# A hand-written step order, chosen anew: each batch's scores placed next to a context product on TensorE

## The chip, the cores and the metric

The kernel runs on one core of one Trainium2 chip. The metric is the device time of one launch in microseconds (us). Three runs of the kernel before took 2436.83, 2435.96 and 2436.95 us; the median is 2436.83. The profile comes from one more execution, which took 2435.67 us as a whole and 2433.9 us from its first to its last instruction (the span).

## What is computed

The input is x, 128 batches of 128 rows and 512 columns, and one 128x128 matrix adj for each batch, all in 32-bit floats. Two layers follow each other:

```
h = relu(layernorm(x))
q, k, v = h Wq + bq, h Wk + bk, h Wv + bv          # 8 heads of 64
attn = softmax((q k^T) / 8 * (2 adj))              # 8 matrices of 128x128 a batch
x = x + (attn v) Wo + bo

h = relu(layernorm(x))
e[i, j] = leaky_relu(h W a_left [i] + h W a_right [j])
att = softmax over i of (e where adj > 0.5, else -9e15)
x = x + elu(att (h W))
```

## The kernel before

**Pairs, groups and units.** The work is cut into 64 pairs of two batches, a and b. Two pairs make a group of four batches; q, k and v are made for a whole group at once. A product with a 512x512 matrix is done in quarters by a scheme with seven block products in the place of eight, with sums and differences of blocks made ahead on VectorE (DVE). For a group this gives 21 *units* (seven each for v, q and k; function `product`, matmuls on line 261), which are spread over two rounds: U1 to U10 of an even pair are v0 v1 v2 v3 v4 q0 v5 q1 v6 q2, U1 to U11 of an odd pair are q3 q4 k0 q5 k1 q6 k2 k3 k4 k5 k6. Some units are read out at once: by a copy or bias step on ScalarE (ACT), called F with the unit's number (lines 273 and 278), or by an add on the DVE, called A (line 282). All units of v (or q, or k) that use bank "a" write the same accumulator one after another, so the next one must wait until the F step has read it. The products of a pair's rows with Wo (steps o0 to o6) and with W (w0 to w6) go the same way on line 302; they are read out by the steps od (DVE, line 400), zc (ACT, line 478) and wd (DVE, line 482).

**The attention of a batch** (letter a or b at the end of the name): `sc` makes the scores on TensorE: 8 products with a contraction of 64, on one half of the array's rows each (line 323; tile 64x128). `at` multiplies them with adj (DVE, line 329), `mx` takes the maxima (line 336), `ex0` to `ex3` are the exponentials of two heads each (ACT, line 341), `rc` the reciprocals (DVE, line 345), `nm0` to `nm3` the normalisation (ACT, line 350). `fl` transposes 32x32 blocks (DVE, line 357), `bl` and `pl` send the blocks out and bring them back in their places by DMA (SyncE's queue, lines 361 and 367), so that `pc` can make the context on TensorE: 8 products with an output of 64 partitions, on one half of the array's columns each (line 386; tile 128x64). `pe` copies the context to SBUF (ACT, line 393), and `cs0` to `cs3` make its block sums (DVE).

**The second layer of a pair:** statistics `st0`, `st1` (DVE), the power `pw` on GpSimd, `nm` (DVE, line 410), the normalised rows `h20`, `h21` (ACT, line 416), four dot products `d00` to `d11` (DVE, line 423), their spread by a transpose `pb` on TensorE (line 432), the mask `wm` (DVE, line 438), `pr`, `m1`, `e1`, `sw` for the softmax, the gather products `g0`, `g1` on TensorE (line 464), their copies `ge0`, `ge1` (ACT, line 470), block sums `gs0` to `gs3` (DVE), then w0 to w6, and at the end `ez`, `fa`, `fb` and the store `so`. The hidden rows of later pairs are made on the DVE by `hd0`, `hd1` and, for a group, the four block sums `hs0` to `hs3` (function `hidden_sum`). `t0`, `t1` and `s0` are the statistics of a later pair's x; `la`, `lt`, `lx`, `l0`, `lT` and `f0` are loads.

**Buffers that matter here.** Six PSUM buffers (pool `ps1`) are shared by the accumulators of the units, the row products, pc, pg and pb; the scores have two banks of their own in one buffer (`ps2`). There is one buffer each for `at`, `tr` and `aT`. A new tile in a buffer waits until the old tile there has been read.

**What sets the order.** Nothing is scheduled by the machine: the list `ORDER` (line 536) is written out, 138 of its steps exist, and each carries a lag. Round p goes through the list from left to right and runs each step for pair p minus its lag, if that step exists for that pair (entries with strange lags, such as A7:-37, are steps that exist for no pair). Each engine works through its own instructions in just this order, and waits where an input isn't ready. So the list sets the order on all engines, and a software pipeline over some five rounds:

```python
for p in range(early, N + late):
    for step, lag in ORDER:
        pair = p - lag
        for do in tables.get(pair, {}).get(step), first_use.get((pair, step)):
```

Of the kernel before, what the change touches and what calls it, by code (L numbers as in the profile page):

```python
# [24 lines left out]
def kernel(  # L25
# [35 lines left out]
    xs, x0s, adjs, adjTs, hAs, hSs = {}, {}, {}, {}, {}, {}  # L61
# [93 lines left out]
    def token_sum(h, s, k):  # L155

        if k == 0:
            nc.vector.tensor_tensor(s[:, 0], h[:, 2], h[:, 3], OP.add)
        elif k == 1:
            nc.vector.tensor_tensor(s[:, 1], s[:, 0], h[:, 0], OP.subtract)  # L160
        elif k == 2:
            nc.vector.tensor_tensor(s[:, 2], h[:, 0], h[:, 2], OP.subtract)
        else:
            nc.vector.tensor_tensor(h[:, 2], h[:, 1], s[:, 1], OP.subtract)
# [16 lines left out]
    st0, rows0, qks, vs, scs, ats, trs, blocks, aTs, pcs = ({} for _ in range(10))  # L181
# [45 lines left out]
            nc.vector.scalar_tensor_tensor(h, h, 0.0, row, op0=OP.max, op1=OP.mult)  # L227

    def hidden_sum(g, k):
        if k == 0:  # L230
            hSs[g] = grp.tile([P, 3, 2, 2 * S], F32, name="hS")
        token_sum(hAs[g], hSs[g], k)

# [288 lines left out]
    def spread_u():  # L522
# [13 lines left out]
    ORDER = [  # L536
        (step.split(":")[0], int(step.split(":")[1]))
        for step in """
        w5:4 o4:2 ata:0 U2:0 w6:4 mxa:0 sw:3 pca:1 od4:2 plb:1 g0:3 zc5:4 o5:2 od4c:2 wd6:4 o6:2 fa:4 exa2:0 hs1:1
        g1:3 exa0:0 ez:4 F2:0 U1:0 ge0:3 U8:1 fb:4 exa1:0 ge1:3 od5:2 od6:2 rca0:0 exa3:0 st0:2 st1:2 gs0:3 t0:0  # L540
        rca1:0 w0:3 nma1:0 U4:0 w1:3 gs2:3 scb:0 pw:2 pcb:1 so:4 A3:20 nm:2 pea:1 t1:0 nma0:0 gs1:3 nma2:0 nma3:0
        gs3:3 zc0:3 h21:2 A8:1 A9:1 fla:0 U11:1 atb:0 h20:2 hs3:1 F4:0 mxb:0 peb:1 F1:0 U3:0 d10:2 o0:1 A11:1 F3:0
        d11:2 A7:-37 A2:0 U5:0 cs0:1 exb0:0 A10:28 f0:0 cs1:1 lT:0 lt:2 exb1:0 F5:0 exb2:0 A4:21 exb3:0 U6:0 rcb0:0
        nmb0:0 F6:0 wd1:3 U7:0 A5:0 F8:-10 F7:0 o1:1 F11:10 cs2:1 l0:-1 d00:2 hd0:0 rcb1:0 s0:0 A1:19 nmb1:0 w2:3
        hd1:0 nmb3:0 zc2:3 pb:2 U9:0 F9:0 hs0:0 lx:1 o3:1 A6:0 d01:2 w4:3 nmb2:0 wm:2 sh:1 bla:0 od0:1 la:-1 pr:2
        U10:0 w3:3 od1:1 o2:1 F10:0 hs2:0 pla:0 flb:0 m1:2 zc4:3 od2:1 sca:-1 blb:0 cs3:1 e1:2 wd4c:3
        """.split()
    ]

    def steps(p):  # L550
# [60 lines left out]
        if odd and (g + 2) * 2 < N:  # L611
            for k in range(4):
                table[f"hs{k}"] = lambda k=k: hidden_sum(g + 2, k)
# [11 lines left out]
    with tc.manual_schedule():  # L625
# [10 lines left out]
        for k in range(4):  # L636
            hidden_sum(0, k)
        for n, u in enumerate(SEQ):
            firsts, adds = product(0, u[0], int(u[1]))
            if n == 2:  # L640
                weight_sums(wq_sb)
            if n == 4:
                first_stats(2)
            if n == 6:
                hidden_T(2, rows[2], "h2")
            if n == 8:
                weight_sums(wk_sb)
            if n == 10:
                first_stats(3)
            if n == 12:  # L650
                hidden_T(3, rows[3], "z")
                load_x0(4)
            if n == 14:
                for k in range(4):
                    hidden_sum(1, k)
            firsts()
            adds()
# [59 lines left out]
```

## Time and profile before

| engine | busy us | share of the 2433.9 us | instructions |
|---|---|---|---|
| TensorE, matmuls (PE) | 2395.6 | 98% | 14264 |
| TensorE, weight loads (PEld) | 2055.1 | 84% | 14264 |
| VectorE (DVE) | 1993.2 | 82% | 3909 |
| ScalarE (ACT) | 1449.3 | 60% | 4811 |
| GpSimd (POOL) | 180.3 | 7% | 323 |

In the profile, PE is TensorE's matmul stream and PEld its weight loads, which run beside it. Each 32-bit matmul shows as two instructions, so a unit of four matmuls is counted x8 and a row product of two x4. The DMA engines are busy 42.7% of the time with the kernel's transfers. The granted TensorE clock is 0.996 of full speed on the mean.

The run has three parts: the head up to some 80 us, in which the first group's products are made and the first pair is worked on alone; rounds of 37.1 us each on the mean; and a tail from about 2326 us, in which no units are left. The first scores of the last pair start at 2350.71 us.

### The profile page before, as it was taken

The numbers are of one execution on the slowest core, as the hardware profiler recorded it, in microseconds if no ns is written. First come the engines' busy times: TensorE is split into PE (matmuls) and PEld (weight loads), VectorE is DVE, ScalarE is ACT, GpSimd is POOL, SyncE is SP. The second block draws the span as 40 slices with busy tenths as digits, with TensorE's granted clock in tenths as the row PEclk, the third lists the DMA queues.
The fourth block names the chain that finished last, engine by engine and source line by source line (L and its number), as shares of the span: only waits on it lengthen the run. The fifth ranks groups of instructions, "written<-read, shape, count | busy, mean of one in ns | idle before, by whom it ended". The sixth has DMA issues, their size and how long they took to land.

```text
span 2433.9 us, 40532 instructions
## 1 busy us (share of the span) xinstructions
PE 2395.6 (98%) x14264; PEld 2055.1 (84%) x14264; DVE 1993.2 (82%) x3909; ACT 1449.3 (60%) x4811; POOL 180.3 (7%) x323
## 2 busy tenths in 40 slices
PE   8999999999999999999999999999999999999987
PEld 7788888888888888888888888888888888888876
DVE  5788888888888888888888888888888888887786
ACT  2566556656565665565665656655656655666573
POOL 1000000000000000000000000000000000000000
PEclk9999999999999999999999999999999999999998
DMA  4435434445343454344453434453444544443331
GB/s 156 122 110 147 129 115 119 137 135 139 113 132 109 142 140 143 101 135 121 135 148 111 133 109 138 135 145 99 139 118 135 148 118 125 116 140 116 104 112 65
DMA packets 255275, 306.09 MB, mean 126 GB/s; under 512 B 21856, under 2 KB 181600, under 8 KB 254432
## 3 DMA queue, kind: packets, MB, share of 16 engines
q1 hardware_dynamic: 251568, 303.37, 42.7%
q8 instruction: 112, 1.84, 0.3%
q14 instruction: 91, 0.75, 0.1%
q0 software_dynamic: 1920, 0.13, 0.1%
q10 hardware_dynamic: 1584, 0.01, 0.0%
HBM read 202.64 MB, written 100.79 MB: 125 GB/s over the span
## 4 chain that ended last, share of the span: by engine, by line
PE 96%; DVE 2%; ACT 1%; issue 0%; DMA 0%; POOL 0%; SPq 0%; POOLq 0%; DVEq 0%; ACTq 0%
PE acc_a L261 27%; PE row_a L302 23%; PE acc_c L261 14%; PE row_c L302 9%; PE acc_b L261 7%; PE sc L323 6%; PE pc L386 5%; PE pg L464 5%; PE pb L432 1%; DVE junk L423 0%; DVE nmx L336 0%; PE pt L202 0%; ACT at L341 0%; DVE st L172 0%; DMA x<-in_x 0%
## 5 line engine op out<-in xcount | busy, mean ns | idle before, releaser
L341 ACT ACTIVATE at<-at,nmx 128x128 f32<-128x128 f32 x1024 | 398.6, 394 | 90.7 <-DVE nmx L336 90.6
L302 PE MATMUL row_a<-w,gT 128*128 128x256 f32 x1280 | 338.5, 388 | 15.1 <-DVE z L482 14.2
L350 ACT ACTIVATE at<-at,rs 128x128 f32<-128x128 f32 x1024 | 331.8, 394 | 0.0
L302 PE MATMUL row_a<-wo,cxT 128*128 128x256 f32 x1280 | 328.8, 380 | 0.1
L302 PEld LDWEIGHTS row_a<-w,gT 128*128 128x128 f32 x1280 | 239.3, 191 | 55.6 <-issue 9.2
L478 ACT COPY z<-row_a 128x256 f32<-128x256 f32 x256 | 94.9, 371 | 301.0 <-PE row_a L302 298.6
L302 PEld LDWEIGHTS row_a<-wo,cxT 128*128 128x128 f32 x1280 | 237.8, 190 | 30.8 <-DVE x L400 0.7
L400 DVE TENSOR_TENSOR x<-row_a,x 128x256 f32<-128x256 f32 x320 | 134.9, 422 | 144.5 <-PE row_a L302 139.8
L329 DVE SCALAR_TENSOR_TENSOR at<-sc,adj 128x1024 f32<-128x1024 f32 x128 | 156.8, 1225 | 98.5 <-PE sc L323 97.3
L278 ACT ACTIVATE kT<-acc_a,bk 128x256 f32<-128x256 f32 x256 | 107.5, 471 | 178.4 <-PE acc_a L261 178.4
L176 POOL TENSOR_SCALAR mv<-mv 128x2 f32<-128x2 f32 x128 | 32.8, 256 | 2196.3 <-ACT at L341 1858.8
L341 ACT ACTIVATION_READ_ACCUMULATOR at<-at,nmx 128x1 f32 x1024 | 195.3, 191 | 0.0
L278 ACT ACTIVATE qT<-acc_a,bq 128x256 f32<-128x256 f32 x256 | 105.7, 463 | 123.6 <-PE acc_a L261 123.6
L172 DVE BATCH_NORM_STATS2 st<-x 128x6 f32<-128x512 f32 x256 | 172.6, 674 | 4.7 <-DMA x<-in_x 4.6
L357 DVE STREAM_TRANSPOSE tr<-at 128x1024 f32<-128x1024 f32 x128 | 158.1, 1235 | 8.4 <-ACT at L350 8.3
L323 PEld LDWEIGHTS sc<-kT,qT 64*128 64x128 f32 x2048 | 124.2, 187 | 42.5 <-issue 42.1
L336 DVE TENSOR_REDUCE nmx<-at 128x8 f32<-128x1024 f32 x128 | 155.9, 1218 | 3.3
L323 PE MATMUL sc<-kT,qT 64*128 64x128 f32 x2048 | 148.7, 285 | 0.0
L464 PE MATMUL pg<-w,h 128*128 128x128 f32 x1024 | 141.2, 281 | 0.0
L464 PEld LDWEIGHTS pg<-w,h 128*128 128x128 f32 x1024 | 129.2, 191 | 14.0 <-issue 10.6
L386 PE MATMUL pc<-aT,v 128*64 128x128 f32 x2048 | 140.1, 279 | 0.0
L273 ACT COPY v<-acc_a 128x512 f32<-128x512 f32 x128 | 75.2, 587 | 104.2 <-PE acc_a L261 103.6
(126 smaller groups left out, 4925.4 us busy)
## 6 DMA issues: line engine op xcount, KB each, us to landing
blocks<-tr SPq DMA_DIRECT2D x128, 512.0 KB, 3.6
aT<-blocks SPq DMA_DIRECT2D x512, 128.0 KB, 2.9
x<-in_x SPq DMA_DIRECT2D x123, 512.0 KB, 6.6
out<-x SPq DMA_DIRECT2D x64, 512.0 KB, 3.8
hA<-in_xT SPq DMA_DIRECT2D x120, 256.0 KB, 4.6
mr<-rows SPq DMA_DIRECT2D x60, 256.0 KB, 4.7
adj<-in_adj SPq DMA_DIRECT2D x64, 128.0 KB, 5.2
adjT<-in_adjT SPq DMA_DIRECT2D x64, 128.0 KB, 4.3
```

The lines of the kernel that those rows point to most:

```text
L172: nc.vector.bn_stats(st, src[:, i, :])
L261: nc.tensor.matmul(acc[:, m, :], lhsT, rhs, start=fresh and m == 0 and c == 0, stop=c == 1, skip_group_check=True)
L278: nc.scalar.activation(dst(t, f)[:, m, :], a[:, m, :], AF.Identity, bias=bias[:, j : j + 1])
L302: nc.tensor.matmul(acc, left[:, la, c, :], w[:, wb, c, :], start=n in (0, 3) and c == 0, stop=c == 1, skip_group_check=True)
L323: nc.tensor.matmul(sc[:, s * C + j, :], qT[r, j, cols], kT[r, j, cols], start=True, stop=True)
L329: nc.vector.scalar_tensor_tensor(at, scs.pop(b), QSCALE, adjs[p][:, i : i + 1, :].to_broadcast([P, H, S]), op0=OP.mult, op1=OP.mult)
L336: nc.vector.tensor_reduce(nmx, at, AX.X, OP.max, negate=True)
L341: nc.scalar.activation(at[:, j, :], at[:, j, :], AF.Exp, bias=nmx[:, j : j + 1], accum_out=sums[:, j : j + 1])
L350: nc.scalar.activation(at[:, j, :], at[:, j, :], AF.Copy, scale=rs[:, j : j + 1])
L357: nc.vector.transpose(trs[b], at.rearrange("p h (j k) -> p j h k", k=Q))
L386: nc.tensor.matmul(pc[s * D : (s + 1) * D, j, :], vs[b // G][:, b % G, head * D : (head + 1) * D], aT[:, :, s * C + j, :], start=True, sto ...
L464: nc.tensor.matmul(pg[:, c, :], h1s[p][0][:, i, c * P : (c + 1) * P], wts[p][:, i, :], start=True, stop=True)
```

## The change

Two things change in the file. `hidden_sum` now makes its tile when the group has none, and no longer at k = 0, so that the four block sums may begin in any order that the list has. And the whole list is another one:

```diff
     def hidden_sum(g, k):
-        if k == 0:
+        if g not in hSs:
             hSs[g] = grp.tile([P, 3, 2, 2 * S], F32, name="hS")
@@
-        w5:4 o4:2 ata:0 U2:0 w6:4 mxa:0 sw:3 pca:1 od4:2 plb:1 g0:3 zc5:4 o5:2 od4c:2 wd6:4 o6:2 fa:4 exa2:0 hs1:1
-        g1:3 exa0:0 ez:4 F2:0 U1:0 ge0:3 U8:1 fb:4 exa1:0 ge1:3 od5:2 od6:2 rca0:0 exa3:0 st0:2 st1:2 gs0:3 t0:0
-        rca1:0 w0:3 nma1:0 U4:0 w1:3 gs2:3 scb:0 pw:2 pcb:1 so:4 A3:20 nm:2 pea:1 t1:0 nma0:0 gs1:3 nma2:0 nma3:0
-        gs3:3 zc0:3 h21:2 A8:1 A9:1 fla:0 U11:1 atb:0 h20:2 hs3:1 F4:0 mxb:0 peb:1 F1:0 U3:0 d10:2 o0:1 A11:1 F3:0
-        d11:2 A7:-37 A2:0 U5:0 cs0:1 exb0:0 A10:28 f0:0 cs1:1 lT:0 lt:2 exb1:0 F5:0 exb2:0 A4:21 exb3:0 U6:0 rcb0:0
-        nmb0:0 F6:0 wd1:3 U7:0 A5:0 F8:-10 F7:0 o1:1 F11:10 cs2:1 l0:-1 d00:2 hd0:0 rcb1:0 s0:0 A1:19 nmb1:0 w2:3
-        hd1:0 nmb3:0 zc2:3 pb:2 U9:0 F9:0 hs0:0 lx:1 o3:1 A6:0 d01:2 w4:3 nmb2:0 wm:2 sh:1 bla:0 od0:1 la:-1 pr:2
-        U10:0 w3:3 od1:1 o2:1 F10:0 hs2:0 pla:0 flb:0 m1:2 zc4:3 od2:1 sca:-1 blb:0 cs3:1 e1:2 wd4c:3
+        atb:1 mxb:1 A1:74 f0:1 gs2:4 A2:1 lT:1 U3:1 h20:3 bla:1 A3:55 gs3:4 A11:2 o0:2 h21:3 d01:3 peb:2 lx:2 F3:1
+        d10:3 exb1:1 w2:4 exb0:1 lt:2 U5:1 F5:1 rcb0:1 U6:1 U7:1 cs2:2 d00:3 cs0:2 exb2:1 zc2:4 exb3:1 pb:3 A5:1
+        rcb1:1 d11:3 wm:3 hd0:1 cs1:2 nmb1:1 w4:4 hd1:1 U8:1 nmb3:1 sh:2 nmb2:1 F7:1 nmb0:1 hs0:1 U9:1 F4:1 A6:1 w3:4
+        o1:2 F6:1 od0:2 zc4:4 pr:3 F9:1 s0:1 pla:1 A7:-33 l0:0 U10:1 w5:4 od1:2 F8:11 m1:3 wd4c:4 F10:1 flb:1 blb:1
+        o2:2 w6:4 e1:3 sca:0 od2:2 cs3:2 pca:1 o4:2 sw:3 wd6:4 F11:3 o3:2 A9:1 pea:1 zc5:4 ata:0 mxa:0 g0:3 od4:2 U2:0
+        ez:4 o5:2 exa3:0 la:0 exa0:0 plb:1 exa2:0 fa:4 ge0:3 hs1:1 od4c:2 g1:3 fb:4 rca1:0 F2:0 od5:2 hs2:1 st0:2
+        exa1:0 nma3:0 A8:1 ge1:3 o6:2 A4:26 rca0:0 w0:3 od6:2 t1:0 w1:3 U1:0 hs3:1 nma0:0 zc0:3 t0:0 A10:84 st1:2
+        nma2:0 nma1:0 gs0:3 so:4 U11:1 scb:0 gs1:3 pw:2 pcb:1 wd1:3 U4:0 fla:0 nm:2 F1:0
```

The two lists begin at different places of a round, so they are easier to compare when each is turned to begin at sca, with lags counted from there. TensorE's steps are then:

```
before: sca w5:4 o4:2 U2 w6:4 pca:1 g0:3 o5:2 o6:2 g1:3 U1 U8:1 w0:3 U4 w1:3 scb pcb:1 U11:1 U3 o0:1 U5 U6 U7 o1:1
        w2:3 pb:2 U9 o3:1 w4:3 U10 w3:3 o2:1
after:  sca pca:1 o4:2 o3:2 g0:3 U2 o5:2 g1:3 o6:2 w0:3 w1:3 U1 U11:1 scb pcb:1 U4 U3 o0:1 w2:3 U5 U6 U7 pb:2 w4:3
        U8 U9 w3:3 o1:1 U10 w5:3 o2:1 w6:3
```

Before, pcb stood behind scb while sca and pca had other products between them; after, both contexts stand right behind scores. U8 runs in its pair's own round and no longer one round later, and w5 and w6 stand at the end of a round where they stood at the start of the next. On the other engines the steps change places as well. The DVE's steps from one sca to the next, after the change, are: od2 cs3 sw wd6 A9 ata mxa od4 fa hs1 od4c fb rca1 od5 hs2 st0 A8 rca0 od6 t1 hs3 t0 st1 gs0 gs1 wd1 fla nm atb mxb gs2 A2 gs3 A11 d01 d10 rcb0 cs2 d00 cs0 A5 rcb1 d11 wm hd0 cs1 hd1 sh hs0 A6 od0 od1 m1 wd4c flb; before, wd1 stood behind d10, d11 and rcb0, and nm ahead of fla. Those of ACT are: pea zc5 ez exa3 exa0 exa2 ge0 F2 exa1 nma3 ge1 nma0 zc0 nma2 nma1 F1 h20 h21 peb F3 exb1 exb0 F5 exb2 zc2 exb3 nmb1 nmb3 nmb2 F7 nmb0 F4 F6 zc4 pr F9 F10 e1; before, too, peb stood behind h20 and h21. What each step computes stays the same.

## The prediction

> **What bounds the kernel now.** I read the page first: TensorE's busy share, then the chain that ended last.
>
> ```profile
> PE 2395.6 (98%) x14264; PEld 2055.1 (84%) x14264; DVE 1993.2 (82%) x3909; ACT 1449.3 (60%) x4811; POOL 180.3 (7%) x323
> ...
> PE 96%; DVE 2%; ACT 1%; issue 0%; DMA 0%; POOL 0%; SPq 0%; POOLq 0%; DVEq 0%; ACTq 0%
> ```
>
> The chain is TensorE for 96% of the span, so only TensorE's own time counts, unless another engine makes it wait. Next, TensorE's waits over the whole run:
>
> ```profile
> PE row_a L302 <- DVE z L482: 14.2, 5, 5.0
> PE pt L202 <- DVE hn L196: 9.1, 2, 8.8
> PE acc_a L261 <- ACT v L273: 5.4, 2, 4.7
> ```
>
> Asked by window, the first of these falls after 2340 us and the others before 130 us. The stretch between is free of waits: the stretches table shows TensorE busy for 74.00 us of every 74, and the timeline repeats every 74.18 us for two rounds (37.09 a round). So there are three parts: a head to about 80 us, 61 rounds bound by TensorE, and a tail from 2326 us.
>
> What a step costs in the middle is read from the difference of two starts, since ends are modelled. Here are TensorE's pieces in one round (start, length, engine, line, operation, count):
>
> ```profile
> 1175.80 1.03 PE L302 MATMUL row_a<-wo,cxT 128*128 128x256 f32 x4
> 1176.76 1.16 PE L323 MATMUL sc<-kT,qT 64*128 64x128 f32 x16
> 1177.85 1.13 PE L302 MATMUL row_a<-w,gT 128*128 128x256 f32 x4
> 1178.82 1.03 PE L302 MATMUL row_a<-wo,cxT 128*128 128x256 f32 x4
> 1179.68 1.89 PE L261 MATMUL acc_a<-hS,wq 128*128 128x256 f32 x8
> 1181.41 1.03 PE L302 MATMUL row_c<-w,gT 128*128 128x256 f32 x4
> 1182.36 1.09 PE L386 MATMUL pc<-aT,v 128*64 128x128 f32 x16
> 1183.39 1.16 PE L464 MATMUL pg<-w,h 128*128 128x128 f32 x8
> 1184.38 1.03 PE L302 MATMUL row_a<-wo,cxT 128*128 128x256 f32 x4
> ...
> 1193.05 1.03 PE L302 MATMUL row_a<-w,gT 128*128 128x256 f32 x4
> 1194.01 1.16 PE L323 MATMUL sc<-kT,qT 64*128 64x128 f32 x16
> 1195.10 1.09 PE L386 MATMUL pc<-aT,v 128*64 128x128 f32 x16
> 1196.12 1.99 PE L261 MATMUL acc_a<-hA,wk 128*128 128x256 f32 x8
> 1197.95 1.03 PE L302 MATMUL row_a<-wo,cxT 128*128 128x256 f32 x4
> ```
>
> The reader is to see: a row product normally takes 0.86 us (1178.82 to 1179.68) and a unit of line 261 takes 1.73. A row product ahead of scores takes 0.96 (1175.80), one behind scores 0.97 (1177.85), one ahead of a context 0.95 (1181.41), and the gather behind a context 0.99 where the other gather of the round takes 0.89. So each border between a full-array product and sc or pc costs 0.10. The second half of the round, where pcb already follows scb, has 0.10 at each outer border and none between: sc 1.09, pc 1.02.
>
> **What the Trainium skill says.** "TensorEngine Tiling (Array Packing)", Key Properties, says that "Changing tiling mode (not just tile) drains the TensorE". The trace agrees that a change costs: 64x128 (sc) and 128x64 (pc) beside 128x128 show the 0.10 above. It doesn't show that all changes cost alike: from sc to pc is a change of mode too, yet pc behind sc starts as late after sc (1.09) as a row product does, and itself loses nothing more. "TensorE: Matmul & The Clock Gate", Step-by-step, says that the next weights are loaded while the present matmul runs. The trace agrees: a row product's weights start 0.2 us ahead of its matmuls, but those of sc, pc and the product behind them start together with theirs.
>
> **The change part by part.** No instruction is added or removed; the new condition in hidden_sum only lets the sums stand in another order. Everything else is place in the queues.
>
> (1) sca and pca meet. Before, apart: 0.10+1.09+0.10 and 0.10+1.03+0.10, 2.52 us. After, like scb and pcb: 0.10+1.09+1.02+0.10, 2.31. That is 0.20 us a round; 61 TensorE-bound rounds give **-12.2**. In the two rounds after, TensorE isn't the bound, so nothing is counted.
>
> (2) The wait of U5 on F3. In even rounds the copy F3 (line 273) ends as U5, v's next unit into the same accumulator, wants to write. Before, one row product stood between U3 and U5, and U5 took 1.81 (1162.55 to 1164.36; two rounds on 1.80) instead of 1.73. After, o0 and w2 stand between, 0.86 more. 30 even rounds by 0.075: **-2.2**.
>
> (3) U8 moves one round earlier. Before, the last U8 ran at 2334.10, where the chain is DVE's; after, it runs in a TensorE-bound round: one more unit on the path, **+1.7**.
>
> (4) The tail. From 2325.6 to 2375.8 the pairs take 25.1 us each, and the DVE's rows for a pair without units add up to about 25 (scores, maxima and transposes 6x1.23, od and wd 10x0.42, token sums 8x0.42, dots 4x0.69, statistics 2x0.8, fa, fb, sh 3x1.23, small ones 2): the DVE is the bound, and its work is unchanged. After that it is a chain of latencies. There w2 waited for wd1, 14.2 us in five waits, since wd1 stood behind the dots; after, wd1 stands right behind gs1. Against this, o0 now waits for peb, which stands behind h20 and h21 on ACT. I can only bound it: all waits on wd1 outside the DVE-bound pairs (1.5+4.4+1.2, about 7) as a gain, and about 4 as a loss, two detours of two h2 rows (2x0.76) and their rest. I take **-2**.
>
> (5) The head. Round 0 waits for U7 behind the constants on the DVE (4.7 us); these hang on the same steps as before. I take 0, bounds -2 and +2.
>
> (6) Does a new wait come up between? With TensorE gapless, its steps have fixed places; I put the measured rows of DVE and ACT behind them in the new order and looked for inputs that come late. The tight ones:
> - pca now takes the accumulator that wd6 frees, in odd rounds. o2 starts 1.82 before sca; od2 starts 1.07 after its product (1176.87 after 1175.80); od2 0.35, cs3 0.33, sw 0.55, wd6 0.42 end 0.90 after sca's start. pca is due at 1.09: 0.2 to spare.
> - U8 takes pb's accumulator, freed by wm. In even rounds, from U5's start: F5 begins at 1.93, and F5, exb2, zc2, exb3, rcb1, d11 take 0.48, 0.78, 0.37, 0.9, 0.1, 0.7, so the DVE is at wm at 5.3. pb starts at 5.18 (three units), wm can start 0.42 later and ends at 6.02; U8 is due at 6.26. 0.2 to spare.
> - o0 needs peb in even rounds: from od2 (0.75 before sca's start) the DVE's rows through nm add up to 17.3 with some 0.6 of gaps between dependent ones; h20, h21 and peb add 2.2, so peb ends at 19.4. o0 is due at 20.1: 0.7 to spare.
> - pca itself comes 4.5 us earlier behind sca than it did. Its aT: fla ends near 16.5 us of the round before, the two transfers land after 3.6 and 1.8+2.9 us (page, part 6), at about 25; pca is due at 38. SP's queue moves past nothing that waits longer: plb waits for pca, which is now earlier; lT waits for U11 (to 14.4) ahead of bla, which waits for fla anyway.
> - The DVE has 61.6 us of work in 73.7, ACT 44.9. Loads (lx, lt, la, l0) move by less than a round, and each has a round's lead.
> So new waits cost 0 in the likely case; both ends for the range: 0 and, for 0.2 us too little at two places in 30 rounds, +6 to the sum after their margins of 0.2 are used up.
>
> Sum: -12.2 -2.2 +1.7 -2 = -14.7 us against the span 2433.9, which gives 2419.2. The profiled run took 2435.67 as a whole and the three timed runs 2435.96 to 2436.95; from the median 2436.83 I get **2422.1**.
>
> **The rivals.**
> (A) As above: 2422.1, own range 2416 to 2428.
> (B) The tail gains all of its 7 and the likely rest stays: 2436.8-12.2-2.2+1.7-7 = 2417. For it: five long waits on one step that moves ahead. Against: the DVE-bound pairs can't shrink.
> (C) The handoffs of (6) with 0.2 to spare, pca behind wd6 and U8 behind wm, turn into waits of 0.2 to 0.4 us in every second round: 30 x (0.2 to 0.4) = 6 to 12 back, 2428 to 2434. For it: 0.2 us is the size of a semaphore's way and of one small DVE row. Against: the before kernel runs with a spare of nothing at F3 and loses only 0.08.
> (D) Slower: o0 behind peb. If h20, which waits for nm behind fla, starts later than summed, peb and o0 come late in even rounds, and TensorE stands. The point: lateness of 0.7 is free, 0.7+14.7/30 = 1.2 eats the gain, 1.35 is 0.2% slower. fla 2 us late (its exponentials and shares alternate between ACT and DVE) gives 30x1.3 = 39 back: 2461. Against: the last normalise ends near 13 us, 2 ahead of fla's turn, so only a slip on the DVE itself does it.
> (E) The order doesn't do what it says: TensorE would pay the border between sc and pc. Excluded by 1194.01 to 1196.12, unless pca waits for data (C).
>
> **How the numbers follow.** A 0.70, B 0.12, C 0.12, D 0.05, E 0.01. About 0.2% (4.9 us, 2432) is what a measurement of this kernel can tell from no change. A and B are faster; of C about half; D is slower. So faster 0.87, same 0.08, slower 0.05. The range 2415 to 2430 takes in A, B and C's better third.
>
> **What would show it.** Right: weight loads of pc that wait for issue in one place only, not 65 (21.5 us now); those of sc as before (127); two rounds in about 73.7 us instead of 74.18; no TensorE wait between 130 and 2300 us; no wait of row_a on z of several us in the tail. Wrong: TensorE waiting for DVE w (line 438), z (482) or ACT cxT (393) some 30 times; a row of 0.10 left at pca's border; a tail longer than before's 83 us behind the last sca.

## The result, and the profile after

Six runs of the changed kernel took 2420.41 to 2422.53 us, 2421.05 in the median; six runs of the kernel before took 2436.89 in the median. The ratio is 0.9936, with a 95% interval of 0.9924 to 0.9949: faster by 15.8 us, where 14.7 were forecast. The profiled span is 2419.4 us, where the sum gave 2419.2. That the total fits this well is partly luck: the middle of the run went as forecast, but one term of the head was incomplete and the tail's was right for a wrong reason.

TensorE's busy share and the chain on the page after:

```profile
PE 2381.3 (98%) x14264; PEld 2063.0 (85%) x14264; DVE 1969.7 (81%) x3909; ACT 1439.4 (59%) x4811; POOL 174.8 (7%) x323
...
PE 96%; DVE 2%; ACT 2%; issue 0%; DMA 0%; POOL 0%; SPq 0%; POOLq 0%; DVEq 0%; ACTq 0%
```

The instructions are the same in number, and TensorE's busy time is 14.3 us less, which is nearly all of the gain: the waits that the profile lists for TensorE add up to 30.7 us before and 30.5 after. What went away was counted as busy: most of it is time at the borders between TensorE's own products, a smaller part a handoff that the list doesn't show (U5's, below). TensorE's pieces after, in one round (start, length, engine, line, operation, count):

```profile
1205.79 1.03 PE L302 MATMUL row_a<-wo,cxT 128*128 128x256 f32 x4
1206.65 1.03 PE L302 MATMUL row_c<-w,gT 128*128 128x256 f32 x4
1207.61 1.16 PE L323 MATMUL sc<-kT,qT 64*128 64x128 f32 x16
1208.70 1.09 PE L386 MATMUL pc<-aT,v 128*64 128x128 f32 x16
1209.72 1.13 PE L302 MATMUL row_a<-wo,cxT 128*128 128x256 f32 x4
1210.69 1.03 PE L302 MATMUL row_c<-wo,cxT 128*128 128x256 f32 x4
1211.55 1.05 PE L464 MATMUL pg<-w,h 128*128 128x128 f32 x8
```

Read the starts: 0.86 between the first two row products, 0.96 to sca (border), 1.09 to pca, 1.02 to o4 (no border between), 0.97 for o4 (border), 0.86 for o3. The weight loads of pc say the same over the whole run (busy, mean ns of one, idle before; first the kernel before, then after):

```profile
L386 PEld LDWEIGHTS pc<-aT,v 128*64 128x64 f32 x2048 | 109.2, 136 | 29.2 <-issue 11.9 <-ACT at L341 9.6
L386 PEld LDWEIGHTS pc<-aT,v 128*64 128x64 f32 x2048 | 109.2, 136 | 15.9 <-issue 0.7
```

For pc the idle time with a name, 21.5 us in 65 places before, is 0.7 in two, the last two contexts, which have no scores ahead of them; all its idle time fell from 29.2 to 15.9. For sc nothing changed (42.1 us on issue in both). TensorE's waits of the whole run (total, times, longest):

```profile
PE pb L432 <- DVE junk L423: 12.2, 4, 4.7
...
PE acc_a L261 <- ACT v L273: 5.4, 2, 4.7
PE row_a L302 <- DVE z L482: 1.9, 2, 1.0
```

Between 130 and 2326 us there is none, as before. In the tail the wait of row_a on z has shrunk from 14.2 to 1.9, and a new one has come up: pb waits for the dots.

This list leaves out handoffs of one or two tenths of a microsecond. The same question put to the weight loads shows them. In the kernel before, between 130 and 2326 us, the only waits of weight loads on another engine, apart from those of pc, are U5's on the copy F3:

```profile
PEld acc_a L261 <- ACT v L273: 6.2, 29, 0.2
```

In the kernel after this one is gone as well, and all that is left of the kind in that stretch is one wait of 0.2 us.

Where the time went is read from the starts of the first scores of a pair (from the timelines, us):

| | sixth pair | 63rd pair | last pair | end |
|---|---|---|---|---|
| before | 212.47 | 2325.58 | 2350.71 | 2433.9 |
| after | 213.49 | 2313.14 | 2340.51 | 2419.4 |
| after less before | +1.02 | -12.44 | -10.20 | -14.5 |

So the head lost 1.0, the 57 rounds between the first two columns gained 13.46, the round behind them lost 2.24 and the rest of the tail gained 4.3. The middle repeats to 0.01 us from round to round; the head and the tail don't. Experiments 5 and 7 have the order of the kernel after up to the sixth pair, and there its scores came at 213.59 and 214.35.

### The profile page after: what moved, and what is told of

It is laid out like the page before. It is cut to its first block, busy times and chain, and to the rows that moved or that the text cites. A ratio compares the mean times of both kernels' runs of the same rounds, so it can differ in the third digit from the quotient of the medians.

```text
span 2419.4 us, 40505 instructions
## 1 busy us (share of the span) xinstructions
PE 2381.3 (98%) x14264; PEld 2063.0 (85%) x14264; DVE 1969.7 (81%) x3909; ACT 1439.4 (59%) x4811; POOL 174.8 (7%) x323
## 4 chain that ended last, share of the span: by engine, by line
PE 96%; DVE 2%; ACT 2%; issue 0%; DMA 0%; POOL 0%; SPq 0%; POOLq 0%; DVEq 0%; ACTq 0%
PE acc_a L261 27%; PE row_a L302 23%; PE acc_c L261 14%; PE row_c L302 9%; PE acc_b L261 7%; PE sc L323 6%; PE pc L386 5%; PE pg L464 5%; PE pb L432 1%; ACT at L341 1%; ACT at L350 0%; DVE junk L423 0%; DVE nmx L336 0%; DVE at L329 0%; PE pt L202 0%
## 5 line engine op out<-in xcount | busy, mean ns | idle before, releaser
L302 PE MATMUL row_a<-wo,cxT 128*128 128x256 f32 x1280 | 336.6, 385 | 0.2
L302 PE MATMUL row_a<-w,gT 128*128 128x256 f32 x1280 | 321.4, 382 | 2.4 <-DVE z L482 1.9
L393 ACT COPY cxT<-pc 128x512 f32<-128x512 f32 x128 | 73.8, 576 | 193.6 <-PE pc L386 193.6
L176 POOL TENSOR_SCALAR mv<-mv 128x2 f32<-128x2 f32 x128 | 27.6, 216 | 2189.1 <-DVE mv L173 2163.0
L323 PEld LDWEIGHTS sc<-kT,qT 64*128 64x128 f32 x2048 | 124.2, 187 | 42.5 <-issue 42.1
L464 PEld LDWEIGHTS pg<-w,h 128*128 128x128 f32 x1024 | 134.2, 191 | 7.1 <-ACT z L478 0.6
L416 ACT ACTIVATE h<-x,nmr,mv 128x512 f32<-128x512 f32 x128 | 97.2, 808 | 64.4 <-DVE nmr L410 64.4
```

The source lines that it names most:

```text
L302: nc.tensor.matmul(acc, left[:, la, c, :], w[:, wb, c, :], start=n in (0, 3) and c == 0, stop=c == 1, skip_group_check=True)
L323: nc.tensor.matmul(sc[:, s * C + j, :], qT[r, j, cols], kT[r, j, cols], start=True, stop=True)
L464: nc.tensor.matmul(pg[:, c, :], h1s[p][0][:, i, c * P : (c + 1) * P], wts[p][:, i, :], start=True, stop=True)
```

## The experiments

**1. The adjacency alone, in the kernel before.** pca needs a free accumulator behind sca, and gets it only if wd6 is done; so w5, w6, wd4c and wd6 stand ahead of sca, at the end of the round. (Here and below, the lines of the list are shown in part.)

```diff
-        w5:4 o4:2 ata:0 U2:0 w6:4 mxa:0 sw:3 pca:1 od4:2
+        o4:2 ata:0 U2:0 mxa:0 sw:3 od4:2
...
-        od4c:2 wd6:4 o6:2
+        od4c:2 o6:2
...
-        zc4:3 od2:1 sca:-1 blb:0 cs3:1 e1:2 wd4c:3
+        zc4:3 od2:1 wd4c:3 w5:3 w6:3 wd6:3 sca:-1 pca:0 blb:0 cs3:1 e1:2
```

> The kernel before with pca moved right behind sca, and with what that needs for a free accumulator: w5, w6, wd4c and wd6 at the end of the round. U8, wd1, F3, U5 and all else stay where the kernel before has them. Theory (each border between sc or pc and a full-array product costs 0.10 us on TensorE): two rounds take 74.18 - 0.40 = 73.78 us, the span is about 2433.9 - 12.2 = 2421.7, give or take 2 for the tail. Rival (the gain came from the new orders on the other engines): two rounds stay at 74.18 and the span near 2434.

Measured: 2450.52 us, ratio 1.006 (1.0045 to 1.0075) to the kernel before: slower. Two rounds took 74.52. Neither side had this. TensorE's pieces show why:

```profile
1217.14 1.03 PE L302 MATMUL row_a<-w,gT 128*128 128x256 f32 x4
1218.15 1.13 PE L302 MATMUL row_c<-w,gT 128*128 128x256 f32 x4
1219.21 1.16 PE L323 MATMUL sc<-kT,qT 64*128 64x128 f32 x16
1220.31 1.09 PE L386 MATMUL pc<-aT,v 128*64 128x128 f32 x16
1221.33 1.13 PE L302 MATMUL row_a<-wo,cxT 128*128 128x256 f32 x4
```

The reader is to see that the border is saved here too (1.10, then 1.02), and that w5 takes 1.01 in place of 0.86 and w6 1.06 in place of 0.96. w6 writes the accumulator that wd4c must have read; wd4c stands behind od2 on the DVE, and od2 waits for o2, two row products ahead of w6. So w6 starts 0.15 late, and takes 0.10 longer itself, as its weights could not be loaded ahead. That is 0.25 in each round; in every second round g1 starts 0.13 late and takes 0.11 longer in the same way. 2x0.25+0.24 = 0.74 lost against 0.40 saved gives 74.18+0.34 = 74.52. The waits of the weight loads between 130 and 2326 us name both handoffs, which TensorE's own list leaves out:

```profile
PEld row_c L302 <- DVE z L482: 22.3, 58, 0.4
PEld pg L464 <- ACT gT L470: 10.7, 29, 0.4
```

The border theory holds, but the adjacency alone loses: in this order the new neighbours on TensorE leave no time for these two handoffs. The middle accounts for 9.8 of the 15.3 us that the span grew; the other 5.5, in the head and the tail, I haven't taken apart.

**2. pca apart again, in the kernel after.**

```diff
-        sca:0 od2:2 cs3:2 pca:1 o4:2 sw:3
+        sca:0 od2:2 cs3:2 o4:2 pca:1 sw:3
```

> The kernel after with pca and o4 exchanged, so that one row product stands between sca and pca; nothing else moves. Theory of borders: two borders more a round, 0.20 us: two rounds take 73.70 + 0.40 = 74.10, the span is about 2419.4 + 12.2 = 2431.6. Rival (the place of pca is of no account): 73.70 and 2419.4.

Measured: 2435.38 us, ratio 0.9997 (0.9989 to 1.0006) to the kernel before; span 2434.2. The rounds took 36.19 and 37.91, 74.10 for two, each 0.20 longer than after. From the sixth to the 63rd pair this is +11.24 us; the head added 1.4 (its first scores were already 0.75 later) and the tail 2.2. So the borders account for 11.2 of the 14.8 us between the two spans; the tail's part goes with short waits that come up there (0.5 us on ge, 0.3 on the transfers of aT) and with a lower granted clock (0.87 for 0.93 in the 25.5 us behind the last pair's first scores), and is not shown to be the borders'. In the middle the exchange of two neighbours costs what the theory says: the rival falls.

**3. w2 behind U5, in the kernel after.**

```diff
-        d10:3 exb1:1 w2:4 exb0:1 lt:2 U5:1 F5:1
+        d10:3 exb1:1 exb0:1 lt:2 U5:1 F5:1 w2:4
```

> The kernel after with w2 moved behind U5 and F5, so that only o0 stands between U3 and U5, as before. Theory (the copy F3 then holds up U5 in every second round): two rounds take 73.70 + 0.075 = 73.775, the span is longer by 2.2: 2421.6. Rival (the 0.075 in two rounds came from elsewhere): 73.70 and 2419.4.

Measured, one run: span 2422.6; two rounds 73.78; from the sixth to the 63rd pair +2.22. The wait of U5's weight loads on F3 is back as it was in the kernel before: 6.2 us in 29 places. As the theory has it.

**4. U8 a round later, in the kernel after.** A8 and A9 must follow it.

```diff
-        hd1:1 U8:1 nmb3:1
+        hd1:1 nmb3:1
...
-        o3:2 A9:1 pea:1
+        o3:2 pea:1
...
-        nma3:0 A8:1 ge1:3
+        nma3:0 ge1:3
...
-        U1:0 hs3:1
+        U1:0 U8:1 hs3:1
...
-        scb:0 gs1:3 pw:2
+        scb:0 gs1:3 A8:1 A9:1 pw:2
```

> The kernel after with U8 and its adds A8 and A9 moved into the next round, U8 behind U1 as before. Theory (a unit in the first round is on the path, the last one in the round that TensorE doesn't bound is not): the sixth pair's first scores start some 1.0 to 1.7 us earlier than after's 213.5, the pair of rounds stays at 73.70, and the tail gives nothing back: span about 2418. Rival (the unit costs its 1.73 us in the tail as well): 2419.4.

Measured, one run: span 2426.5. From the first to the second pair's first scores it took 29.53 in place of 30.88, so 1.35 of the unit's 1.73 is saved in the first round. But the sixth pair's first scores came 1.0 later than after's, at 214.51, and not earlier: the first scores of all came 0.46 later, the round from the third pair to the fourth lost 1.2 (32.04 for 30.84: a wait of 0.94 on the DVE's x and the 0.1 behind it), the one from the second to the third 0.6. Two rounds in the middle took 73.82 for 73.70 (a unit's weight loads now wait for ACT's kT, in 30 places), and the round to the last pair's scores 30.17 for 27.37. Neither side of the expectation is clean, since A8 and A9 moved with it. What does follow: in this order the late U8 isn't hidden in the tail. In the round ahead of the last pair's scores pb waits 4.62 us where it waited 3.54, on top of the unit itself.

**5. The dots that pb reads, first.**

```diff
-        atb:1 mxb:1 A1:74 f0:1 gs2:4 A2:1 lT:1 U3:1 h20:3 bla:1 A3:55 gs3:4 A11:2 o0:2 h21:3 d01:3 peb:2 lx:2 F3:1
-        d10:3 exb1:1
+        atb:1 mxb:1 h20:3 h21:3 d00:3 d10:3 A1:74 f0:1 gs2:4 A2:1 lT:1 U3:1 bla:1 A3:55 gs3:4 A11:2 o0:2 peb:2 lx:2 F3:1
+        exb1:1
...
-        cs2:2 d00:3 cs0:2
+        cs2:2 d01:3 cs0:2
```

> The kernel after with h20, h21 and the two dots that pb reads (d00, d10) moved on the DVE to right behind mxb, ahead of gs2, A2, gs3, A11, d01, rcb0 and cs2; d01 takes the old place of d00. Theory (in the tail's last four rounds TensorE stands at pb until the DVE has got through what is queued ahead of d00, and then runs at a lower clock): pb can start some 2.5 us earlier in the two rounds with scores and about 0.7 to 1.4 earlier in the two behind them; its waits of 12.2 us shrink to under 5, the drop of the clock goes, and the tail from the last pair's scores on and the round ahead of it together get 4 to 9 us shorter: span about 2413, between 2410 and 2416. The middle stays at 73.70 for two rounds. Rival (those rounds are the DVE's anyway, as the prediction had it): the wait moves to another step and the span stays within 1 us of 2419.4.

Measured: 2419.44 us; ratio to the kernel before 0.9932 (0.9919 to 0.9946); span 2417.2. The middle stayed the same to 0.01 us a round. In the tail:

```profile
PE pb L432 <- DVE junk L423: 5.1, 7, 2.1
PE row_a L302 <- ACT z L478: 2.5, 3, 1.0
...
PE row_a L302 <- DVE x L400: 1.7, 1, 1.7
PE row_c L302 <- DVE z L482: 1.1, 1, 1.1
```

pb's wait fell from 12.2 to 5.1, but only 2.2 us reached the span, less than expected: w4 now waits for zc2 (row_a on ACT's z, 1.0 us in two rounds), and others follow. Nor did the drop of the clock go: behind three shorter waits (0.34, 0.48 and 1.03 us) it was 0.51 from 2330.85 to 2334.36. Both had a part: the wait was real, and most of it moved on.

**6. U8 directly behind pb: what a missed handoff costs.**

```diff
-        w4:4 hd1:1 U8:1 nmb3:1
+        U8:1 hd1:1 w4:4 nmb3:1
```

> The kernel after with U8 and w4 exchanged, so that U8 stands directly behind pb, whose accumulator it takes. Theory (U8 had 0.2 us to spare in the kernel after, because wm starts 0.42 after pb and takes 0.42; a TensorE step that had to wait costs 0.10 on top, since its weights were not loaded ahead): due 0.22 after pb's start it gets its accumulator at 0.90, so each round loses 0.68 + 0.10: two rounds take 73.70 + 1.56 = 75.26, the span is about 2466. Rival (the handoff isn't that tight, wm is done sooner): 73.70 and 2419.4.

Measured, one run: span 2465.7; two rounds 75.26. In the timeline:

```profile
1257.25 0.38 PE L432 MATMUL pb<-ident,ws 128*128 128x128 f32 x2
1258.14 1.99 PE L261 MATMUL acc_b<-hA,wq 128*128 128x256 f32 x8 [0.51 <-DVE w L438]
1259.97 1.03 PE L302 MATMUL row_a<-w,gT 128*128 128x256 f32 x4
```

U8 starts 0.89 after pb, where 0.90 was summed from wm's rows, and takes 1.83, 0.10 more than a unit whose weights were loaded ahead. The bracket names 0.51 of it; the start times show all of 0.67, as matmul ends are modelled. So in the kernel after, where w4 puts U8 1.08 behind pb, it had about 0.2 us to spare.

**7. zc2 earlier as well.** To the edit of experiment 5 is added:

```diff
-        exb1:1 w2:4 exb0:1
+        exb1:1 w2:4 zc2:4 exb0:1
...
-        exb2:1 zc2:4 exb3:1
+        exb2:1 exb3:1
```

> The run with the two dots first, and zc2 moved on ACT from behind exb2 to behind exb1. Theory (in the tail w4 now waits for zc2, 1.0 us in two rounds, behind exponentials of 0.8 us each): zc2 comes two of them, 1.6 us, earlier, w4 waits no more, and the two rounds get 1 us shorter each: span about 2415, between 2413.5 and 2416.5; the middle stays at 73.70. Rival (ACT is the bound there, whatever stands first): 2417.

Measured: 2419.03 us; ratio to the kernel before 0.9928 (0.9915 to 0.9942); span 2416.9, with two rounds at 73.70. The wait on ACT's z is 2.5 us still, one of them 2.06 long; it stands at the next row product on w's accumulator. The rival's number is nearer, but that ACT is the bound isn't shown by it. The kernels of experiments 5 and 7 have the lowest medians of all, but their intervals overlap that of the kernel after, and the kernel before, timed beside them, was also 0.8 and 1.7 us lower than beside the kernel after. What sets them apart is the stretch from the 63rd pair's first scores to the end: 103.96 and 102.9 us, where the kernel after has 106.26 and experiments 3 and 6, with its order there, 106.5 and 106.6.

**8. wd1 alone earlier, in the kernel before.**

```diff
-        nmb0:0 F6:0 wd1:3 U7:0
+        nmb0:0 F6:0 U7:0
...
-        hs3:1 F4:0 mxb:0 peb:1
+        hs3:1 F4:0 mxb:0 wd1:3 peb:1
```

> The kernel before with wd1 alone moved on the DVE, from behind d10, A11, d11, A2, cs0, cs1 and rcb0 to right behind mxb. Theory (the tail's waits of w2, 14.2 us in all, are the place of wd1 in the DVE's queue): w2 waits under 4 us, and the tail behind the last pair's first scores falls from 83.2 us to 78 or less. Rival (w2's wait only hides the next one: pb stands right behind w2 and needs d00, which still stands behind all of that work): pb takes over most of the 14.2, and the tail stays within 1.5 us of 83.2. Both: two rounds in the middle stay at 74.18.

Measured, one run: span 2433.9, and 82.8 us behind the last pair's first scores, where the kernel before has 83.2. TensorE's waits on the DVE there:

```profile
PE row_a L302 <- DVE z L482: 6.6, 3, 2.7
...
PE pb L432 <- DVE junk L423: 4.3, 3, 2.0
PE pb L432 <- DVE rs L345: 2.3, 1, 2.3
```

w2 waits 7.6 us less and pb 6.6 more: the rival is right about the tail, w2's wait covered the next one. Only about half of the 14.2 moved, though; the theory had w2 under 4, and it still waits 6.6.

## Why the prediction was right, and where it wasn't

**(1) Borders, right.** Forecast 0.20 a round: the rounds went from 36.18 and 37.99 to 35.99 and 37.71. Experiment 2 puts back 0.20 in each by one exchange.

**(2) U5 behind F3, right.** Forecast 0.075 in every second round; experiment 3 shows 0.08 and 2.22 us, with the wait on F3 by name. U5 didn't start late for it: its weights started 0.03 us ahead of its matmuls in place of 0.2, and it took 1.80 for 1.73. (1) and (2) together give 57x0.20+28.5x0.075 = 13.5 for the stretch that measured 13.46.

**(3) U8 a round earlier: the right sign, the size only roughly shown, and incomplete.** Forecast +1.7. From the first to the second pair's first scores it took 30.88 us, for 29.19 before; experiment 4, with U8 late, has 29.53. But the kernel of experiment 8, which is the kernel before up to there, has 30.42: after the 4.7 us wait of U7 the granted clock was 0.53 for 3.44 us in one trace and 0.54 for 6.46 us in the other. And w5 and w6 also stand a round earlier, which the sum left out: the round from the fourth pair to the fifth went from 34.46 to 35.99, two row products less one round's borders (1.73-0.20). The rounds from the second to the fourth pair gave 0.79 and 0.71, the one from the fifth to the sixth 0.28, as in the middle, and the first scores of all came 0.42 earlier. The net at the sixth pair was +1.0, where the term and four rounds of borders (1.7-0.8) would give +0.9. As no product is added, w5 and w6 of the last pairs are then missing from the tail; what that gave there isn't shown. That the last U8 was free in the tail before is not shown; in the order after it isn't free (experiment 4).

**(4) The tail, right sum, wrong picture.** Forecast -2; from the 63rd pair's first scores to the end it measured 106.26 for 108.32, -2.06. But the picture of the DVE as the bound doesn't hold for the kernel after. These are the stretches between the first scores of the 63rd and the last pair, before and after, and a part of the latter (length; busy us of PE, PEld, DVE, ACT and POOL, with instructions; granted clock, DMA share, GB/s):

```profile
2325.58:2350.71 25.13, 22.93 (x155) 18.70 (x154) 23.75 (x50) 17.66 (x63) 1.03 (x2) 1.00 0.35 111
2313.14:2340.51 27.37, 23.82 (x148) 19.56 (x147) 23.36 (x49) 18.40 (x65) 1.09 (x2) 0.88 0.40 115
2331.80:2337.40 5.60, 5.60 (x14) 4.53 (x15) 2.76 (x7) 3.09 (x10) 0.00 (x0) 0.50 0.06 10
```

Before, the DVE was busy for 23.75 of 25.13 us, so the bound was near there. After, it has no more work (23.36) and the stretch is 2.24 longer. This is the part ahead of pb, from after's chain of waits (start, length, engine, tile and line):

```profile
2328.30 0.42 DVE gT L164
2328.72 0.60 DVE kT L282
2329.32 0.62 DVE junk L423 x2
...
2330.03 0.70 DVE junk L423 x2
...
2331.13 0.62 DVE junk L423 x2
...
2331.80 0.69 PE pb L432 x2
```

The DVE runs through gs, A11 and d01 before d10 and d00, which pb needs, and TensorE stands for 3.54 us. Then the granted clock is 0.50 for 5.6 us: three row products take 1.7 us each in place of 0.86, and the DVE waits for them in its turn (3.1 us at od0). An estimate from these figures: U8 gone -1.73, borders -0.20, the wait 3.54 for 2.20 before +1.34, half the clock for 5.6 us +2.8, together +2.2. So the slow clock costs more here than the longer wait. It isn't the same in every run: experiments 3 and 6 have TensorE's order of the kernel after in this stretch and the same wait of 3.54, and took 26.27, with the clock at 0.62 for 4.5 us from pb on. In the tails of the traces before and after, the waits of 3.54 to 4.99 us (and one of 2.29) were followed by row products of 1.7 us or more, those of 1.50, 1.65 and 2.20 us were not. I had priced a new wait of o0 on peb as the tail's loss; o0 never waited, and pb did. Experiment 8 shows in the kernel before that taking away half of w2's wait brings pb's out, and experiments 5 and 7 that taking away over half of pb's brings out the next.

**(5) The head's wait for U7** stayed (4.7 us in both). **(6) No new wait in the middle, right:** TensorE's list is empty from 130 to 2326 us, and, since that list leaves out short handoffs (experiment 1), so is that of the weight loads but for 0.2 us. How close that was, experiments 1 and 6 show: the 0.2 us to spare at U8 is real, and a handoff missed by 0.15 costs 0.25. Rival D's price was of that kind; at its place, peb, nothing waited.

What isn't settled: where the 0.79 and 0.71 us of the head's two rounds come from, how much of the tail's gain is waits and how much the clock, and whether the last U8 cost anything in the tail before. In the runs with the order of the kernel after, the second pair's first scores moved by up to 0.9 us (83.52 to 84.38) between kernels that are alike up to there, so questions of a microsecond in the head need many runs.

## What to carry to other kernels

Where TensorE is busy for 98% of the span, look at the starts of its pieces and not at its waits: what lies between a product's normal length and its length at a change of tile shape is paid in every round, and here sc and pc, standing together, saved two of four borders. Ask for the waits of the weight loads too, since they name short handoffs that TensorE's own list leaves out. Then check each handoff that the new neighbours bring closer, buffer by buffer, against rows of the profile, because here one that came 0.15 us late cost its lateness and 0.10 for the lost loading of weights on top. In a tail, the longest wait is not what a fix is worth: here another stood right behind it, and the products after a long wait ran at half the clock.

## What the runs showed that was not expected

A TensorE step that starts late takes 0.10 us longer as well: 1.83 for 1.73 in experiment 6, 1.06 for 0.96 in experiment 1. It is the same 0.10 as at a change of tile shape, and in both cases the weights start together with the matmuls and not 0.2 ahead; U5 before, whose weights had 0.03 us, lost 0.07. And the change from the 64x128 shape of sc to the 128x64 shape of pc adds nothing in any of the runs: sc takes 1.09 and pc 1.02 whether they stand together or not. As the weights of pc start together with its matmuls behind sc too (1208.70 for both), what costs the 0.10 at the other borders isn't shown to be the late weights alone.
